# Half-row Toeplitz products of two images side by side, with even and odd lags under one weight tile

## The chip, the cores and the metric

The kernel runs on one core of one Trainium2 chip. The metric is the device time of the whole kernel in microseconds (us). Times of single instructions are given in nanoseconds (ns). All data are f32.

The engines are TensorE (PE; its weight loads are listed apart as PEld), VectorE (DVE), ScalarE (ACT), GpSimd (POOL) and SyncE (SP, which here only issues transfers).

## The reference

Eight images of 128 channels and 32 x 32 pixels go through two layers. Layer 0 is an attention over rows and then a spectral unit along the 1024 pixels taken as a sequence. Layer 1 is a deformable convolution of three taps and then a mixture of eight experts. The part that matters here is the spectral unit. Cut to its core, it is

```python
# u: (8 images, 1024 tokens, 128 channels), normalised; phi: 16 filters over time
U_plus[k]  = causal_convolution(phi[:, k], u)
U_minus[k] = sgn * causal_convolution(phi[:, k], u * sgn)      # sgn = +1, -1, +1, ...
out = sum_k sigma[k] ** 0.25 * (U_plus[k] @ Mpp[k] + U_minus[k] @ Mpm[k])
out = out + sum_lag shift(u, lag) @ Mu[lag]                      # three lags
# four such outputs with their own matrices, over the first 1024, 512, 256 and 128 tokens,
# added with weights from a softmax
```

The alternating sign splits a convolution by the parity of the lag. The sum of the two paths is the convolution with the even lags, taken with the matrix Mpp + Mpm, and the convolution with the odd lags, taken with Mpp - Mpm. An output token of one parity gets its even lags from input tokens of the same parity and its odd lags from the other parity. So all of it is done on sequences of 512 tokens: one parity of one image each.

## The kernel before

**The stages.** The attention comes first (`attention_bounded`; about the first 1018 us of the profiled execution), then a short preparation, and then `spectral_and_second_layer`, to the end. The latter works through four groups of two images. For each group it runs the 16 filters, and between the products it places steps of other work: the second layer of the group before (`layer.image`) and the normalisation of the next group (`spec.prepare`). The images of the last group have their second layer at the end, alone.

**The order is written out by hand.** In `spectral_and_second_layer` each engine executes in the order in which the Python code emits. The other work is a generator, `behind`; each `next` on it emits one step, and it is advanced 1.8 times (`RATE`) at each of eight places per filter. Each filter's products run while the products of the filter before are mixed.

**One filter's products** (`filter_image`, L1148 to L1158). The filter lies in SBUF as a Toeplitz tile `teto` of 128 rows: row p, column c holds phi[p + c - 127] of one parity of lags (L1045 to L1055). The 512 columns for the even lags come first and the 513 for the odd lags behind them. For one image, one output parity (`par`) and one parity of lags (`term`), four matmuls accumulate in one PSUM bank `pu`: the weights are the 128-token block i of the normalised input `ur`, and the moving operand is the first 512 - 128 i columns of the filter, written to the columns from 128 i on. So the matmuls have 512, 384, 256 and 128 columns. In each of them the first 128 columns are the diagonal block of the Toeplitz matrix, half of which is zeros: among these, one quarter is a whole block of 64 x 64 zeros. ScalarE then copies the bank to `us` (L1158). The pool of `pu` has two banks, used in turn.

**The mixing** (`mix`, L1160 to L1165, through `add`, L1141). The copied product of the filter before is multiplied by the filter's 128 x 128 matrices and accumulates in `po`, four banks that hold a group's sums over all filters. The matrices differ over four stretches of tokens (`SPANS`), so a mix has four matmuls with 2 x 64, 2 x 64, 2 x 128 and 2 x 256 columns, of two images at once.

**A round.** One filter is four rounds: (par, term) = (0,0), (0,1), (1,0), (1,1). Within a round the order on TensorE is: product of the first image, the three short spans of the mix, steps of other work, product of the second image, the long span, steps of other work. Each round has its own `us` tile (a pool of six).

**The preparation of a group** (`prepare`, L1083 to L1113). For each image: an indirect DMA from GpSimd's queue fetches the tokens, VectorE takes their statistics, GpSimd computes the inverse deviation in 13 small instructions, VectorE writes the normalised tokens `ur`, and TensorE transposes them for the three lags of `Mu`. For the first group all of it lies ahead of the first product.

Of the kernel before, what the change touches and what calls it, by code (L numbers as in the profile page):

```python
# [9 lines left out]
F32 = mybir.dt.float32  # L10
# [6 lines left out]
P = 128  # L17
B = 8
C = 128
T = 1024  # L20
NT = T // P
HT = T // 2
# [3 lines left out]
NF = 16  # L26
# [5 lines left out]
PHI_ROW = PHI_PAD + 1 + HT  # L32
GROUPS = ((0, 1), (2, 3), (4, 5), (6, 7))
RATE = 1.8
# [3 lines left out]
SPANS = ((0, 64, 4), (64, 128, 3), (128, 256, 2), (256, 512, 1))  # L38
# [613 lines left out]
def norm_steps(nc, sb, src, dst, eps):  # L652

    st = sb.tile([P, NT, 6], F32, tag="st", name="st", bufs=2)
    mv = sb.tile([P, NT, 2], F32, tag="mv", name="mv", bufs=2)
    for i in range(NT):
        nc.vector.bn_stats(st[:, i, :], src[:, i, :])
        nc.vector.bn_aggr(mv[:, i, :], st[:, i, :])
        if i % 2:
            yield  # L660
    rs = inverse_std(nc, sb, mv[:, :, 1], eps)
    for _ in range(3):
        yield
    for i in range(NT):
        nc.vector.tensor_scalar(
            dst[:, i, :], src[:, i, :], mv[:, i, 0:1], rs[:, i : i + 1],
            ALU.subtract, ALU.mult,
        )
        if i % 4 == 3:
            yield  # L670


class DeformAndExperts:
# [90 lines left out]
    def bank(self, name):  # L764
        return self.ps.tile([P, 512], F32, tag="ps", name=name)
# [244 lines left out]
class Spectral:  # L1010
# [34 lines left out]
    def load_filter(self, k):  # L1045


        t = self.sb.tile([P, 2 * HT + 1], F32, tag="teto", name="teto", bufs=3)
        self.nc.sync.dma_start(
            t[:, 0:HT], bass.AP(self.phi_e.tensor, k * PHI_ROW, [[1, P], [1, HT]])  # L1050
        )
        self.nc.sync.dma_start(
            t[:, HT:], bass.AP(self.phi_o.tensor, k * PHI_ROW, [[1, P], [1, HT + 1]])
        )
        return t[:, 0:HT], t[:, HT:]  # L1055

    def load_matrices(self, k, first):

# [25 lines left out]
    def prepare(self, group, bank):  # L1084

        nc, sb = self.nc, self.sb
        for n, b in enumerate(group["images"]):
            if n == 0:
                group["x1"], group["ur"] = [], []
                ut = group["ut"] = sb.tile([C, 2, 2, HT + 1], F32, tag="ut", name="ut")  # L1090
                nc.gpsimd.memset(ut[:, :, :, 0:1], 0.0)
            x1 = sb.tile([P, NT, C], F32, tag="x1", name="x1", bufs=2)
            nc.gpsimd.indirect_dma_start(
                out=x1.rearrange("p i c -> p (i c)"), out_offset=None,
                in_=self.x1d.rearrange("b p i c -> (b p) (i c)"),
                in_offset=bass.IndirectOffsetOnAxis(ap=self.back[:, b : b + 1], axis=0),
            )
            ur = sb.tile([P, NT, C], F32, tag="ur", name="ur", bufs=4)
            group["x1"].append(x1)
            group["ur"].append(ur)  # L1100
            yield
            yield
            yield from norm_steps(nc, sb, x1, ur, 1e-5)
            yield
            for par in range(2):
                pt = bank("p_ut")
                for i in range(4):
                    nc.tensor.matmul(
                        pt[:, i * P : (i + 1) * P], ur[:, par * 4 + i, :], self.flip,
                        start=True, stop=True,  # L1110
                    )
                nc.scalar.copy(ut[:, n, par, 1 : HT + 1], pt)
                yield  # L1113
# [30 lines left out]
        )  # L1144
        group["opened"].add(bank)

    def filter_image(self, group, n, par, term, teto, us):

        nc = self.nc
        src = par if term == 0 else 1 - par  # L1150
        flt = teto[0] if term == 0 else teto[1][:, par : par + HT]
        pu = self.up.tile([P, HT], F32, tag="u", name="pu")
        for i in range(4):
            nc.tensor.matmul(  # L1154
                pu[:, i * P : HT], group["ur"][n][:, src * 4 + i, :], flt[:, 0 : HT - i * P],
                start=(i == 0), stop=(i == 3),
            )
        nc.scalar.copy(us[:, n, :], pu)  # L1158

    def mix(self, group, par, term, spans, mf, us, last):  # L1160
        for lo, hi, k in spans:
            self.add(
                group, (par, lo // 256), self.span(group, par, lo, hi), mf[:, k - 1, term, :],
                us[:, 0 : len(group["images"]), lo:hi], last and term == 1,
            )  # L1165

    def finish(self, group):
# [9 lines left out]
def spectral_and_second_layer(tc, spec, layer):  # L1177
    groups = [{"images": im} for im in GROUPS]
    for _ in spec.prepare(groups[0], layer.bank):
        pass  # L1180
    work = [(g, k) for g in range(len(groups)) for k in range(NF)]
    loaded = {}

    def load(n):
        if n < len(work):
            g, k = work[n]
            loaded[n] = spec.load_filter(k), spec.load_matrices(k, g == 0)

    behind, done, todo = iter(()), 0, 0.0
    load(0)  # L1190
    load(1)
    before = None
    for n in range(len(work) + 1):
        now = work[n] if n < len(work) else None
        if now is not None and now[1] == 1:

            g = now[0]
            tasks = [layer.image(b, groups[g - 1]["x2"][:, m]) for m, b in
                     enumerate(groups[g - 1]["images"])] if g else []
            if g + 1 < len(groups):  # L1200
                tasks.append(spec.prepare(groups[g + 1], layer.bank))
            behind = chain(*tasks)
        sums = {}
        for i in range(4):
            par, term = divmod(i, 2)
            if now is not None:
                group = groups[now[0]]
                us = spec.sb.tile([C, 2, HT], F32, tag="us", name="us", bufs=6)
                sums[i] = us
            for m in range(2):  # L1210
                if now is not None and m < len(group["images"]):
                    spec.filter_image(group, m, par, term, loaded[n][0], us)
                if before is not None and before[1] == 0 and i + m == 0:
                    spec.start_sums(groups[before[0]])
                if before is not None:
                    spec.mix(
                        groups[before[0]], par, term, SPANS[0:3] if m == 0 else SPANS[3:4],
                        loaded[n - 1][1], kept[i], before[1] == NF - 1,
                    )
                todo += RATE  # L1220
                while todo >= 1:
                    todo -= 1
                    next(behind, None)
        if before is not None and before[1] == NF - 1:
            for _ in behind:
                pass
            spec.finish(groups[before[0]])
        load(n + 2)
        kept, before = sums, now
    runs = [layer.image(b, groups[-1]["x2"][:, m]) for m, b in enumerate(groups[-1]["images"])]  # L1230
    alive, step = [], 0
    while runs or alive:
        if runs and step % STAGGER == 0:
            alive.append(runs.pop(0))
        alive = [r for r in alive if next(r, r) is not r]
        step += 1
# [3 lines left out]
def metaformer_kernel(  # L1240
# [33 lines left out]
    with tc.manual_schedule(engines=None):  # L1274
        spectral_and_second_layer(tc, spec, layer)
# [50 lines left out]
```

## Time and profile before

| | us |
|---|---|
| median of three runs | 3162.05 |
| lowest and highest | 3161.14, 3165.78 |
| span of the profiled execution | 3164.1 |
| TensorE busy | 2788.8 |
| of it the products, L1154 | 1206.0 |
| of it the mixing, L1142, with `us` and `mf` | 530.6 |
| ScalarE, copies of the products, L1158 | 299.6 |

The table is from the first part of the page (busy time of each engine) and from its fifth (groups of instructions by line). Each f32 matmul of the program is executed as two instructions, each with its own load of weights, so counts of instructions are twice those in the code: L1154 has 2048 matmuls and 4096 instructions. The mean granted clock of TensorE was 0.951. The first product starts at 1060.66 us, and the last product's records start at 2918 us.

The array form of a matmul is printed ahead of its shape: 128*128 uses the whole array, 64*128 half of its rows, 32*128 a quarter of its rows, 128*32 a quarter of its columns.

### The profile page before, as it was taken

The numbers are of one execution on the slowest core, as the hardware profiler recorded it, in microseconds if no ns is written. First come the engines' busy times: TensorE is split into PE (matmuls) and PEld (weight loads), VectorE is DVE, ScalarE is ACT, GpSimd is POOL, SyncE is SP. The second block draws the span as 40 slices with busy tenths as digits, with TensorE's granted clock in tenths as the row PEclk, the third lists the DMA queues.
The fourth block names the chain that finished last, engine by engine and source line by source line (L and its number), as shares of the span: only waits on it lengthen the run. The fifth ranks groups of instructions, "written<-read, shape, count | busy, mean of one in ns | idle before, by whom it ended". The sixth has DMA issues, their size and how long they took to land.

```text
span 3164.1 us, 45167 instructions
## 1 busy us (share of the span) xinstructions
PE 2788.8 (88%) x18888; PEld 1709.7 (54%) x18888; DVE 1430.6 (45%) x2908; ACT 977.2 (31%) x1152; POOL 958.0 (30%) x876
## 2 busy tenths in 40 slices
PE   5898998998997699999999999989899989899154
PEld 2454454454553466666566566656566656566022
DVE  1677778777787320000243531153332144241477
ACT  2665656666664121111212112211212211211100
POOL 1666666666775210000210300120200030200331
PEclk9999999999999799999999999999999999999566
DMA  0000000000000422221520611331611241510541
GB/s 24 8 8 8 15 3 14 15 2 8 9 8 14 119 67 61 72 62 40 154 73 30 204 40 60 119 108 34 197 36 54 87 140 47 170 57 14 159 133 40
DMA packets 176724, 198.76 MB, mean 63 GB/s; under 512 B 17205, under 2 KB 135157, under 8 KB 176513
## 3 DMA queue, kind: packets, MB, share of 16 engines
q1 hardware_dynamic: 160000, 141.26, 15.0%
q0 software_dynamic: 16512, 54.54, 5.8%
q8 instruction: 150, 2.46, 0.3%
q14 instruction: 62, 0.50, 0.0%
HBM read 127.83 MB, written 67.92 MB: 62 GB/s over the span
## 4 chain that ended last, share of the span: by engine, by line
PE 80%; ACT 7%; DVE 7%; issue 3%; DMA 1%; POOL 1%; SPq 1%; another core or an unknown queue 1%; POOLq 0%; DVEq 0%; ACTq 0%
PE pu L1154 35%; PE po L1142 16%; PE s L509 9%; ACT e L514 6%; PE av L561 4%; PE p_e L927 3%; PE z L530 3%; DVE x L909 2%; PE rb L544 2%; PE p_g L856 1%; PE pk L478 1%; DVE x L933 1%; PE pq L464 1%; DVE e L551 1%
## 5 line engine op out<-in xcount | busy, mean ns | idle before, releaser
L1154 PE MATMUL pu<-teto,ur 128*128 128x512 f32 (+3 forms) x4096 | 1206.0, 438 | 53.5 <-issue 42.3
L1154 PEld LDWEIGHTS pu<-teto,ur 128*128 128x128 f32 x4096 | 779.3, 192 | 606.2 <-issue 417.4
L1158 ACT COPY us<-pu 128x512 f32<-128x512 f32 x512 | 299.6, 585 | 1351.2 <-PE pu L1154 1199.0
L523 POOL TENSOR_TENSOR t<-e 128x1024 f32<-128x1024 f32 x256 | 607.0, 2372 | 356.3 <-ACT e L514 354.1
L551 DVE TENSOR_TENSOR e<-e,rb 128x2048 f32<-128x2048 f32 x256 | 569.6, 2281 | 119.3 <-PE rb L544 119.3
L514 ACT ACTIVATE e<-s 128x2048 f32<-128x2048 f32 x256 | 480.8, 1878 | 277.3 <-PE s L509 255.0
L1142 PE MATMUL po<-us,mf 128*128 128x128 f32 (+2 forms) x2048 | 530.6, 382 | 0.0
L509 PE MATMUL s<-q,k 32*128 32x256 f32 x4096 | 301.1, 409 | 75.9 <-ACT e L514 75.7
L894 POOL DMA_INDIRECT g<-tab,cn_idx x192 | 184.9, 963 | 438.6 <-DMA teto<-in_phi_e 240.8
L643 POOL TENSOR_SCALAR rs_v<-rs_v 128x8 f32<-128x8 f32 x24 | 5.9, 246 | 1020.3 <-DVE rs_b L641 1020.3
L509 PEld LDWEIGHTS s<-q,k 32*128 32x128 f32 x4096 | 188.9, 188 | 203.0 <-ACT e L514 165.8
L561 PE MATMUL av<-e,vt 128*32 128x256 f32 x4096 | 277.6, 389 | 4.0 <-DVE e L551 2.7
L1142 PEld LDWEIGHTS po<-us,mf 128*128 128x128 f32 x2048 | 272.0, 193 | 4.1 <-issue 3.9
L909 DVE SCALAR_TENSOR_TENSOR x<-g,w,x 128x128 f32<-128x128 f32 x704 | 248.0, 352 | 51.3 <-DVE x L909 24.2
L933 DVE SCALAR_TENSOR_TENSOR x<-p_e,gates,x 128x128 f32<-128x128 f32 x512 | 177.1, 350 | 171.2 <-PE p_e L927 154.6
L561 PEld LDWEIGHTS av<-e,vt 128*32 128x32 f32 x4096 | 107.9, 110 | 136.4 <-issue 76.3
L537 DVE RECIPROCAL r<-z 128x256 f32<-128x256 f32 x64 | 112.4, 1757 | 98.4 <-PE z L530 98.1
L927 PE MATMUL p_e<-ew,tc 128*128 128x512 f32 x256 | 137.5, 650 | 15.8 <-DVE x L933 12.7
L1076 DVE TENSOR_SCALAR mf<-both,coef 128x256 f32<-128x256 f32 x16 | 5.6, 353 | 290.8 <-PE po L1142 246.2
L530 PE MATMUL z<-t,group 128*32 128x256 f32 x2048 | 135.4, 382 | 0.0
L878 DVE TENSOR_TENSOR om<-p_om,base 128x72 f32<-128x72 f32 x8 | 1.9, 231 | 240.3 <-PE p_om L873 240.3
L1174 DVE COPY x<-po 128x512 f32<-128x512 f32 x8 | 5.5, 692 | 221.3 <-ACT x L1174 221.3
(199 smaller groups left out, 1607.5 us busy)
## 6 DMA issues: line engine op xcount, KB each, us to landing
tab<-gs SPq DMA_DIRECT2D x192, 256.0 KB
mf<-mfd SPq DMA_DIRECT2D x48, 512.0 KB
teto<-in_phi_o SPq DMA_DIRECT2D x64, 256.5 KB
teto<-in_phi_e SPq DMA_DIRECT2D x64, 256.0 KB
mfd<-mf SPq DMA_DIRECT2D x16, 512.0 KB
xc<-in_x SPq DMA_DIRECT2D x8, 512.0 KB
x1d<-xt SPq DMA_DIRECT2D x8, 512.0 KB
mp<-in_M_plus SPq DMA_DIRECT2D x16, 256.0 KB
```

What stands on the lines that cost most here:

```text
L509: nc.tensor.matmul(s[:, j, c, :], img["k"][rows, hg, 2 * r + c, :], q[rows, qc * QU : (qc + 1) * QU], start=True, stop=True,)
L514: nc.scalar.activation(e.rearrange("p j c q -> p (j c q)"), s.rearrange("p j c q -> p (j c q)"), AF.Exp, scale=float(HD) ** -0.5,)
L523: nc.gpsimd.tensor_add(t, e[:, :, 0, :], e[:, :, 1, :])
L530: nc.tensor.matmul(un["z"][32 * j : 32 * j + 32, 0:QU], group, un["t", r][:, j, :], start=(r == 0), stop=(r == 3), skip_group_check=True,)
L551: nc.vector.tensor_tensor(e, e, un["rb"].unsqueeze(2).to_broadcast([P, NH, 2, QU]), ALU.mult)
L561: nc.tensor.matmul(qrt["av"][32 * j : 32 * j + 32, 0:QU], img["v"][:, 2 * r + c, P * hg + 32 * j : P * hg + 32 * j + 32], un["e", r][:, j, ...
L909: nc.vector.scalar_tensor_tensor(x3[:, i, :], g[:, k * C : (k + 1) * C], w[:, i, tap, k : k + 1], (tok if tap + k == 0 else x3)[:, i, :], ...
L927: nc.tensor.matmul(pe, tc[:, i * P : (i + 1) * P], self.ew[:, grp * 4 : grp * 4 + 4, :].rearrange("d e c -> d (e c)"), start=True, stop=True,)
L933: nc.vector.scalar_tensor_tensor(x3[:, i, :], pe[:, k * C : (k + 1) * C], gate[:, i, grp * 4 + k : grp * 4 + k + 1], x3[:, i, :], ALU.mult ...
L1142: self.nc.tensor.matmul(out, lhsT, rhs, start=bank not in group["opened"], stop=last, skip_group_check=True)
L1154: nc.tensor.matmul(pu[:, i * P : HT], group["ur"][n][:, src * 4 + i, :], flt[:, 0 : HT - i * P], start=(i == 0), stop=(i == 3),)
L1158: nc.scalar.copy(us[:, n, :], pu)
```

## The change

A product is no longer made for one image, one output parity and one parity of lags, but for one image, one *source* parity and both parities of lags: the same block of `ur` as weights, and as moving operand a view of `teto` with two stretches of columns, the even lags and the odd lags. The first gives output of the source's own parity, the second output of the other parity. So that both stretches have one distance, the tile is one column longer. A bank `pu` holds 2 x 256 columns: both terms, of one half of the 512 tokens. So a unit (`filter_unit`) is made per source parity and half, four per filter, and each makes both images.

Within each diagonal block the first 64 output columns need 64 of the 128 rows only. These are now matmuls of half height, 2 x 64 columns each. For the second image of a group they use rows 64 to 127 of `ur` and of `teto`. For the first image a copy of rows 64 to 127 of its `ur` is kept in rows 0 to 63 of a new tile `low`, which GpSimd writes once per group, and `teto` is read 64 columns further on in rows 0 to 63, where the same values stand. So the two images' half-height matmuls use different halves of the array's rows and different banks. The remaining columns of each bank get matmuls of full height. A unit's order on TensorE is four half-height matmuls (block, image: first, second, first, second), then the full ones of the first image, steps of other work, the full ones of the second image, steps of other work, and then both mixes, the short spans and the long, of one term of the filter before.

Per filter there were 32 product matmuls with 10240 columns. There are now 24 of full height with 8192 columns and 16 of half height with 128 columns each. The copies by ScalarE stay eight per filter at 512 columns. The mixes, and the number of places for steps of other work, stay. `us` is now one tile per source parity with both terms (a pool of three at twice the size).

```diff
     def load_filter(self, k):
-        t = self.sb.tile([P, 2 * HT + 1], F32, tag="teto", name="teto", bufs=3)
+        t = self.sb.tile([P, 2 * HT + 2], F32, tag="teto", name="teto", bufs=3)
...
+                group["low"] = sb.tile([64, NT, C], F32, tag="low", name="low", bufs=2)
...
             yield from norm_steps(nc, sb, x1, ur, 1e-5)
             yield
+            if n == 0:
+                nc.gpsimd.tensor_copy(group["low"], ur[64:P])
...
-    def filter_image(self, group, n, par, term, teto, us):
+    def filter_unit(self, group, src, half, filters, us):
         nc = self.nc
-        src = par if term == 0 else 1 - par
-        flt = teto[0] if term == 0 else teto[1][:, par : par + HT]
-        pu = self.up.tile([P, HT], F32, tag="u", name="pu")
-        for i in range(4):
-            nc.tensor.matmul(
-                pu[:, i * P : HT], group["ur"][n][:, src * 4 + i, :], flt[:, 0 : HT - i * P],
-                start=(i == 0), stop=(i == 3),
-            )
-        nc.scalar.copy(us[:, n, :], pu)
+        lags = filters[:, 0 : 2 * (HT + 1 - src)].rearrange("p (a c) -> p a c", a=2)
+        images = range(len(group["images"]))
+        pus = [self.up.tile([P, 2, HT // 2], F32, tag="u", name="pu") for _ in images]
+        for i in (2 * half, 2 * half + 1):
+            to = (i % 2) * P
+            for n in images:
+                low = group["low"][0:64] if n == 0 else group["ur"][n][64:P]
+                rows, c0 = (slice(0, 64), 64) if n == 0 else (slice(64, P), 0)
+                nc.tensor.matmul(
+                    pus[n][:, :, to : to + 64], low[:, src * 4 + i, :],
+                    lags[rows, :, c0 : c0 + 64], start=(i % 2 == 0), stop=False,
+                    skip_group_check=True,
+                )
+        for n in images:
+            for i in range(2 * half + 2):
+                to = (i % 2) * P + 64 if i // 2 == half else 0
+                c0 = to + (2 * half - i) * P
+                nc.tensor.matmul(
+                    pus[n][:, :, to:], group["ur"][n][:, src * 4 + i, :],
+                    lags[:, :, c0 : c0 + HT // 2 - to], start=False, stop=(i == 2 * half + 1),
+                    skip_group_check=True,
+                )
+            nc.scalar.copy(us[:, :, n, half * (HT // 2) : (half + 1) * (HT // 2)], pus[n])
+            yield
...
+        for src in range(2):
+            if now is not None:
+                sums.append(spec.sb.tile([C, 2, 2, HT], F32, tag="us", name="us", bufs=3))
+            for half in range(2):
+                unit = iter(())
+                if now is not None:
+                    unit = spec.filter_unit(groups[now[0]], src, half, loaded[n][0], sums[src])
+                for m in range(2):
+                    next(unit, None)
+                    todo += RATE
+                    while todo >= 1:
+                        todo -= 1
+                        next(behind, None)
                 if before is not None:
-                    spec.mix(
-                        groups[before[0]], par, term, SPANS[0:3] if m == 0 else SPANS[3:4],
-                        loaded[n - 1][1], kept[i], before[1] == NF - 1,
-                    )
+                    group = groups[before[0]]
+                    if before[1] == 0 and src + half == 0:
+                        spec.start_sums(group)
+                    for spans in (SPANS[0:3], SPANS[3:4]):
+                        spec.mix(
+                            group, src, half, spans, loaded[n - 1][1], kept[src],
+                            before[1] == NF - 1,
+                        )
```

## The prediction

> **What bounds the kernel now.** I read the page first: the busy line, the slices and the chain.
>
> ```profile
> PE 2788.8 (88%) x18888; PEld 1709.7 (54%) x18888; DVE 1430.6 (45%) x2908; ACT 977.2 (31%) x1152; POOL 958.0 (30%) x876
> ...
> L1154 PE MATMUL pu<-teto,ur 128*128 128x512 f32 (+3 forms) x4096 | 1206.0, 438 | 53.5 <-issue 42.3
> ```
>
> TensorE is busy 88% of the span, and the row of the Toeplitz products, L1154, is the largest. The chain of waits gives 35% of the span to L1154 and 16% to L1142, the mixing matmuls. Cut into stretches, the stage that the change touches runs from 1060 to 2915 us, and TensorE is busy 1799 of these 1855 us. Here time is the sum of what TensorE executes, plus some waits, all in L1154. The timeline of TensorE in one quiet filter, with the start and the length of each merged run:
>
> ```profile
> 1303.57 1.04 PE L1142 MATMUL po<-us,mf 128*128 128x128 f32 x6
> 1304.45 2.32 PE L1154 MATMUL pu<-teto,ur 128*128 128x512 f32 x8
> 1306.61 1.02 PE L1142 MATMUL po<-us,mf 128*128 128x512 f32 x2
> ```
>
> Start to start, one call of filter_image takes 2.16 us (1304.45 to 1306.61), the short mix 0.88, the long mix 0.86. The lengths are larger because their ends overlap the next run. Each f32 matmul appears as two instructions, so 2 x 1280 columns took 2.16 us: 0.844 ns per column and instruction. A filter is four rounds of two calls and two mixes: 24.2 us, of which 8 x 2.156 = 17.25 us is L1154. The work is 64 filters.
>
> The change makes half-height matmuls in this stage, which has none. The attention stage has some (L544, array form 64*128), between 128*32 before and 128*128 after:
>
> ```profile
> 265.30 1.07 PE L561 MATMUL av<-e,vt 128*32 128x256 f32 x16
> 266.30 1.13 PE L544 MATMUL rb<-r,spread 64*128 64x256 f32 x8
> 267.37 1.12 PE L464 MATMUL pq<-hk,wq 128*128 128x512 f32 x2
> ```
>
> The eight of L544 start in four pairs, 7 ns apart within a pair, one on each half of the rows. Four pairs at 256 x 0.844 = 0.216 us are 0.864 us, but the next form starts 1.07 us after them: 0.206 us is extra. And the two 512-column instructions of L464 last 1.12 us together where L1142's last 1.02: 0.10 extra. Start times of single instructions, over all changes of form in the trace with nothing else to wait for, split this: 92 to 96 ns from the end of the last stream to the first load of weights in the new form, and then 107 ns in which this first load is not hidden. The 48 changes from 64*128 to 128*128 have a median of 93 ns.
>
> **What the Trainium skill says.** "TensorEngine Tiling (Array Packing)", section Key Properties: a change of tiling mode drains TensorE. The trace agrees, with the 92 to 96 ns. "TensorE: Matmul & The Clock Gate", section LDWEIGHTS: a load takes its columns over 1.2 GHz, whatever its rows, so 107 ns for 128. The trace agrees: 107 ns exposed for 32, 64 and 128 rows alike. The same page, Part 3: matmuls on different row groups run at the same time, and a load overlaps a running matmul only if its row group differs or it goes to the background buffer. The pairs of L544 agree.
>
> **The change part by part.** *Columns.* Before, each of 8 calls per filter streams 512+384+256+128 = 1280 columns: 10240. After, per source half and image, the full-height matmuls have 512 columns in half 0 (384+128) and 1536 in half 1 (512+512+384+128); times two images and two sources: 8192. The half-height ones have 128 columns and pair up over two images: 4 per unit, 4 units, so 16, or 8 pairs of 128, 1024 columns of time. Total 9216: 1024 fewer columns x 2 instructions x 0.833 ns (the bare stream: a 512-column step takes 0.429 us, a 128-column step 0.109, and the difference is 0.320 for 384 columns) = 1.71 us per filter, 109 us for 64. This is what the change gives if nothing else is added.
>
> *Changes of form.* Each unit enters 64*128 and leaves it. In: 93 ns drain above the usual step, plus 104 of load. Out: 96 (with the 7 ns stagger of the pair) plus 104. Sum 0.40 us per unit, 1.59 per filter. The step from 128*128 into 64*128 itself isn't in the trace; from 128*128 to 32*128 and from 128*32 to 64*128 both show it, so I take their value.
>
> *Sum of the stream.* After: 8192 x 2 x 0.833 ns = 13.65, 48 instructions with 2.6 to 5 ns between = 0.16; 16 pair steps at 0.112 us (128-column steps of L1142 take 0.109 to 0.112) = 1.79; form changes 1.59. Sum 17.19 against 17.25: 0.06 to 0.08 us less per filter, 5 us in 64. With pair steps of 0.107 to 0.118 us and changes of 0.38 to 0.42 us per unit, it lies between 13 us less and 6 more. So the saving and the drains cancel.
>
> *Slack of the two pu banks.* Before, a call takes one bank, and the bank is wanted again after two mixes and another call, 3.9 us. After, a unit's half-height pairs write both banks first, so it waits for ScalarE's copy of the second image, which ends 0.90 us after that image's last matmul starts (1306.49 to 1307.39). Two mixes, 1.74 us, hide that, except in the first filter of all, which has none: four waits of about 0.75, 3 us. But where ScalarE is late, the hiding fails:
>
> ```profile
> 1572.50 2.32 PE L1154 MATMUL pu<-teto,ur 128*128 128x512 f32 x8
> 1574.65 1.04 PE L1142 MATMUL po<-us,mf 128*128 128x128 f32 x6
> 1582.53 4.36 PE L1154 MATMUL pu<-teto,ur 128*128 128x512 f32 x8 [6.83 <-issue]
> ```
>
> The copy due near 1571.9 ran at 1581.89 (ScalarE idle 12.45 us, "issue"), and TensorE ran on for 3.9 us before it stopped. Ten such waits of over 2 us lie between 1090 and 2915. With the change TensorE runs on for 1.74 us when the second image's copy is late, or about 3.5 when the first's is and it must then wait for both copies: 1.1 to 2.2 us worse each. Ends 0 and 22 us; I take 8, as some delays will fall beside other waits.
>
> *Places of the other layer's steps.* Same number (8 places, 14.4 steps per filter), but the places were 3.03 us apart and are now from 0.86 us (two images in half 0) to about 5. TensorE and ScalarE are in order, so a step put 0.86 us after the one that it needs may hold them. Before, no wait of this kind shows in the stage. Ends 0 and 12; I take 4.
>
> *The low copy and the start.* For the first group it stands on GpSimd's queue ahead of the second image's fetch. Before: fetch at 1042.74, first image normalised at 1047.00, second image's statistics from 1049.20, first product at 1060.66. After: the copy can't start before 1047.00; I price 64x1024 at 1.5 us, between the 0.96 of a 128x1024 memset and the 2.34 of an addition. The fetch then follows at 1048.5 and, with the first image's 4.7 us from fetch to statistics, the second's start near 1053.2: 4 us later (ends 3 and 6). In groups 2 to 4 it hides behind some 450 us of products.
>
> *Boundaries, buffers.* Opening a group's sums waited three times 0.70 us for L1174's copies; a whole unit now stands ahead: minus 1 (ends minus 2, 0). Eight ScalarE copies of 585 ns per filter and the loads remain, behind TensorE's 24 us; us keeps its 24 KB per row.
>
> Total: -5 +3 +8 +4 +4 -1 = +13 us on the profiled 3164.1. The unprofiled median is 3162.05, so 3175.
>
> **The rivals.** *Exact balance.* Late copies and crowded steps cost nothing: -5 +3 +4 -1, near 3163. For it: in the stretch 1090 to 1524 TensorE idles under 1 us of 434. Against: the ten waits. *Cheaper changes of form (faster).* TensorE loads the first weights of the new form while the old one still streams, as it does within a form. Half-height loads touch half of the rows only, which speaks for it; the 48 changes out of 64*128 with 107 ns exposed speak against it. If both loads are hidden, a unit saves 0.21 us, 256 units 53 us: 3175 - 53 = 3122. It wins over the lost slack from about 0.05 us per unit, a change priced under 0.35 instead of 0.40. *Pairs in series.* The half-height matmuls of the two images don't overlap: 0.45 us more per unit, 115 us: 3290. L544's pairs, in the same order of halves, speak against it.
>
> **How the numbers follow.** Forecast (slack lost) 0.58, exact balance 0.21, cheaper changes 0.13, series 0.08. About 0.2%, 6 us, is what a measurement can tell from no change. Faster is the third case, 0.13; same the second, 0.21; slower the first and last, 0.66. The forecast's own range is -10 to +44: 3152 to 3206. Adding the balance, and the near end of the third case, 3146 to 3206 leaves out about 2 in 10.
>
> **What would show it.** In the quiet stretch after the first filter, a filter should again take 24.1 to 24.2 us. A unit should show pairs 7 ns apart, 0.09 us of nothing and 0.107 us of bare load on both sides. The idle time ahead of the half-height matmuls should be 10 to 20 us above the 53.5 of L1154, with the ScalarE copy as its releaser. The first product should start near 1064.7. A filter of 23.4 us or less in the quiet stretch would prove the price of the changes wrong; one of 26, the pairs.

## The result and the profile after

The changed kernel takes 3204.59 us (median of four runs, 3195.70 to 3208.97) against 3161.60 for the kernel before (four runs, 3159.01 to 3165.78). The ratio is 1.0131, with a 95% interval of 1.0107 to 1.0155: 43 us slower. The profiled execution spans 3194.0 us, 29.9 more than that of before, and is the fastest of the four.

The page of the changed kernel, parts 1 and 5: busy time, then the groups of the products (matmuls in the last three lines).

```profile
PE 2791.2 (87%) x19912; PEld 1636.8 (51%) x19912; DVE 1427.4 (45%) x2908; ACT 973.8 (30%) x1152; POOL 962.8 (30%) x880
...
L1175 PE MATMUL pu<-teto,ur 128*128 128x384 f32 (+2 forms) x3072 | 977.1, 464 | 0.0
...
L1166 PE MATMUL pu<-teto,low 64*128 64x128 f32 x1024 | 188.5, 303 | 44.4 <-issue 39.0
L1166 PE MATMUL pu<-teto,ur 64*128 64x128 f32 x1024 | 185.4, 302 | 23.4 <-issue 22.3
```

TensorE is as busy as before, with 1024 instructions more. The full-height products, L1175, never wait. All idle time of the products stands before the half-height ones, L1166, which open each unit. There are 67.8 us of it (44.4 + 23.4), where L1154 had 53.5. The changes of form are not in it: in a quiet filter, below, no idle time is shown beside them, because the modelled end of each matmul reaches over the change.

The timeline of TensorE in one quiet filter of the changed kernel (start, length, merged run; of the second and the third pair the first line alone):

```profile
1300.64 0.37 PE L1166 MATMUL pu<-teto,low 64*128 64x128 f32 x1
1300.65 0.37 PE L1166 MATMUL pu<-teto,ur 64*128 64x128 f32 x1
1300.86 0.27 PE L1166 MATMUL pu<-teto,low 64*128 64x128 f32 x1
1300.97 0.27 PE L1166 MATMUL pu<-teto,low 64*128 64x128 f32 x1
1301.08 0.27 PE L1166 MATMUL pu<-teto,low 64*128 64x128 f32 x1
1301.09 0.27 PE L1166 MATMUL pu<-teto,ur 64*128 64x128 f32 x1
1301.29 5.43 PE L1175 MATMUL pu<-teto,ur 128*128 128x512 f32 x16
1306.56 1.90 PE L1146 MATMUL po<-us,mf 128*128 128x128 f32 x8
1308.39 0.37 PE L1166 MATMUL pu<-teto,low 64*128 64x128 f32 x1
```

The pairs run side by side. The first pair takes 0.22 us to the next, the others 0.11: the first load of weights is bare. After the last pair 0.20 us pass to L1175, for 0.107 us of stream, and the mixes take 1.83 us where 0.88 + 0.86 = 1.74 stood before: both are the drain. Over the entries with no other wait (some 250 of 256) the median time from the end of the last stream to the new form is 95 ns, and the bare load is 106 ns. On the way out it is 94 and 106. A quiet filter takes 24.13 us from start to start, and it took 24.21.

So the stream of work is where it was, and the 30 us must be elsewhere. The next table cuts the profiled executions by the starts of instructions in the trace: the attention ends with the start of its last L561 matmul, a filter goes from its first product to the next filter's first product, and the last row begins with the start of the last mixing matmul. "Gather filters" are the 12 filters in which the second layer of the six images of groups 1 to 3 fetches its rows (two per image); in a kernel without waits they take as long as quiet ones. The two columns on the right are for later: they are the same two programs in the experiments, on two different chips (the kernel before on chip 12, the changed one on chip 10).

| us | before | after | difference | before, chip 12 | after, chip 10 |
|---|---|---|---|---|---|
| to the end of the attention | 1015.7 | 1012.4 | -3.4 | 1013.0 | 1013.3 |
| from there to the first product | 44.9 | 53.2 | +8.3 | 44.5 | 53.6 |
| first filter | 17.3 | 19.4 | +2.1 | 17.8 | 20.5 |
| 14 quiet filters | 339.0 | 337.8 | -1.2 | 339.0 | 337.8 |
| 12 gather filters | 367.3 | 391.8 | +24.5 | 290.6 | 289.6 |
| the other 37 filters | 1141.4 | 1144.5 | +3.1 | 1141.4 | 1144.5 |
| after the last mix | 238.3 | 234.9 | -3.4 | 231.9 | 232.8 |
| span | 3164.1 | 3194.0 | +29.9 | 3078.2 | 3092.0 |

Most of the loss is in the gather filters, where the kernel before already lost 77 us against quiet ones. The longest case in the changed kernel, TensorE and then ScalarE:

```profile
2280.59 2.00 PE L1175 MATMUL pu<-teto,ur 128*128 128x384 f32 x8
2282.43 1.90 PE L1146 MATMUL po<-us,mf 128*128 128x128 f32 x8
2299.06 0.79 PE L1166 MATMUL pu<-teto,low 64*128 64x128 f32 x2 [14.73 <-issue]
```
```profile
2279.31 0.58 ACT L1180 COPY us<-pu 128x512 f32<-128x512 f32 x1 [3.73 <-remote]
2298.43 1.29 ACT L1180 COPY us<-pu 128x512 f32<-128x512 f32 x2 [18.53 <-remote]
```

ScalarE makes no copy from 2279.9 to 2298.43, and then both of the unit at once. TensorE finishes the unit and the mixes by 2284.3 and stands still for 14.73 us. The profile puts the wait down to "issue", but it ends at 2299.06, when the first of the two copies (0.58 us, from 2298.43) has just ended. Summed over the stage (waits of TensorE between 1090 and 2835 us: total us, times, longest us), first the kernel before, then the changed one:

```profile
PE pu L1154 <- issue: 42.3, 9, 8.4
PE pu L1154 <- ACT us L1158: 11.2, 3, 8.6
```
```profile
PE pu L1166 <- issue: 61.3, 10, 14.7
PE po L1146 <- issue: 8.1, 7, 2.3
PE pu L1166 <- ACT us L1180: 5.4, 1, 5.4
```

Before the products 53.5 us became 66.7, which is 13.2 more. Another 8.1 us stand before mixing matmuls. They lie inside two runs of mixes (2079.9 to 2084.1 and 2578.4 to 2584.7 us), whose matmuls start 1.4 to 2.8 us apart there. No bank is waited for: ScalarE executes nothing from 2069.9 to 2089.9 or from 2569.9 to 2589.9 us, and these mixes go on without it. So whatever held ScalarE may have held TensorE too. Without the waits, the gather filters took 313.8 us before (367.3 - 53.5) and 317.0 after (391.8 - 74.8), against 290.6 and 289.6 in the two columns on the right: 23.2 and 27.4 us went into slower running. The clock is lower there: between 1560 and 1610 us the granted clock was 0.90 in the kernel before and 0.86 in the changed one. So the 24.5 us are 13.2 and 8.1 of waits, 4.2 of slower running, and 1.0 less of stream.

### The profile page after: what moved, and what is told of

It is laid out like the page before. It is cut to its first block, busy times and chain, and to the rows that moved or that the text cites. A ratio compares the mean times of both kernels' runs of the same rounds, so it can differ in the third digit from the quotient of the medians.

```text
span 3194.0 us, 47045 instructions
## 1 busy us (share of the span) xinstructions
PE 2791.2 (87%) x19912; PEld 1636.8 (51%) x19912; DVE 1427.4 (45%) x2908; ACT 973.8 (30%) x1152; POOL 962.8 (30%) x880
## 4 chain that ended last, share of the span: by engine, by line
PE 57%; DVE 5%; issue 3%; another core or an unknown queue 1%; SPq 1%; DMA 1%; POOL 0%; ACT 0%; POOLq 0%; DVEq 0%; ACTq 0%
PE pu L1175 29%; PE po L1146 16%; PE pu L1166 5%; PE p_e L927 3%; DVE x L909 2%; DVE x L933 2%; PE p_g L856 1%; SPq L864 1%; PE p_turn L772 1%; PE p_l L971 0%; PE p_out L944 0%; PE p_out L947 0%; PE p_ut L1112 0%; DMA g<-tab,cn_idx 0%
## 5 line engine op out<-in xcount | busy, mean ns | idle before, releaser
L1175 PE MATMUL pu<-teto,ur 128*128 128x384 f32 (+2 forms) x3072 | 977.1, 464 | 0.0
L1175 PEld LDWEIGHTS pu<-teto,ur 128*128 128x128 f32 x3072 | 537.7, 192 | 437.5 <-issue 273.6
L1146 PE MATMUL po<-us,mf 128*128 128x128 f32 (+2 forms) x2048 | 490.4, 382 | 8.1 <-issue 8.1
L1146 PEld LDWEIGHTS po<-us,mf 128*128 128x128 f32 x2048 | 294.2, 192 | 42.1 <-issue 28.4
L561 PE MATMUL av<-e,vt 128*32 128x256 f32 x4096 | 276.6, 388 | 5.5 <-DVE e L551 4.2
L1166 PEld LDWEIGHTS pu<-teto,low 64*128 64x128 f32 x1024 | 136.0, 189 | 238.4 <-issue 229.4
L1166 PE MATMUL pu<-teto,low 64*128 64x128 f32 x1024 | 188.5, 303 | 44.4 <-issue 39.0
L1166 PE MATMUL pu<-teto,ur 64*128 64x128 f32 x1024 | 185.4, 302 | 23.4 <-issue 22.3
L561 PEld LDWEIGHTS av<-e,vt 128*32 128x32 f32 x4096 | 107.7, 110 | 137.0 <-issue 75.1
L1166 PEld LDWEIGHTS pu<-teto,ur 64*128 64x128 f32 x1024 | 135.6, 190 | 26.1 <-issue 24.0
```

The lines of the kernel that those rows point to most:

```text
L561: nc.tensor.matmul(qrt["av"][32 * j : 32 * j + 32, 0:QU], img["v"][:, 2 * r + c, P * hg + 32 * j : P * hg + 32 * j + 32], un["e", r][:, j, ...
L1146: self.nc.tensor.matmul(out, lhsT, rhs, start=bank not in group["opened"], stop=last, skip_group_check=True)
L1166: nc.tensor.matmul(pus[n][:, :, to : to + 64], low[:, src * 4 + i, :], lags[rows, :, c0 : c0 + 64], start=(i % 2 == 0), stop=False, skip_g ...
L1175: nc.tensor.matmul(pus[n][:, :, to:], group["ur"][n][:, src * 4 + i, :], lags[:, :, c0 : c0 + HT // 2 - to], start=False, stop=(i == 2 * h ...
```

## Experiments

My theory was that the stream balances, as the quiet filters show, and that the loss is slack: a unit needs both banks of `pu` at its start, so TensorE runs on for a shorter time when a ScalarE copy is late. The rival was that steps of other work, which now stand 0.9 to 5 us apart and not 3 us, hold TensorE and ScalarE throughout. The start was a matter of its own.

The experiments ran on two chips, 10 and 12, on which the kernel before takes 3079 to 3081 us and has none of the long waits. So each is compared with runs of the kernel before on its own chip. Which chip the first comparison ran on is not known, nor whether another chip or another occasion made the 80 us between the two levels.

### Without the gathers

```diff
-                g = sb.tile([P, 4 * C], F32, tag="g", name="g", bufs=9)
-                nc.gpsimd.indirect_dma_start(out=g, in_=rows, in_offset=...)
-                fetched[i].append(g)
+                fetched[i].append(self.still)
```

`still` is a tile that a memset fills once.

The kernel before:

> The kernel before without the 192 indirect gathers of the second layer: VectorE reads a tile filled once instead, so the sampled values are left out. All theories: TensorE's ten long waits (about 50 us between 1090 and 2915 us) lie in the gather phases. If the gathers make ScalarE's copies late, they vanish and the time falls by 50 to 75 us, to about 3090 to 3110. If something else makes them late (fetching of instructions, VectorE), they stay and the time falls by less than 20.

The changed kernel:

> The changed kernel without the same 192 gathers (the sampled values are left out). Lost slack: the difference to the kernel before without gathers is only what the rest of the prediction's sum gives, -5 stream, +5 start, +3 first filter, at most +4 crowded places, so 2 to 8 us instead of about 40. Crowded places as the main cost: the difference stays at 25 us or more.

The kernel before without gathers took 3062.28 us, 0.9944 (0.9927 to 0.9960) of its 3079.18. The changed kernel without them took 3071.48. The first expectation failed. The 17 us come from the end of the kernel (210.2 us after the last mix against 231.9), less a start that is 6.4 us longer (50.9 against 44.5), and the 12 gather filters take 290.6 us with gathers and without. On this chip the gathers cost the products nothing, so this run can't tell what makes ScalarE late in the first comparison. The second expectation was missed by a little: the distance is 9.2 us (expected 2 to 8, and 25 or more for the rival). The run alone doesn't decide against the rival, as there were no long waits to take away. What does is the row of the other 37 filters in the table: there the changed kernel takes 3.1 us more, in the first comparison and in the experiments alike, where the stream alone gives 3.0 less. So crowded places cost about 6 us there, and they are not the main cost.

### The changed kernel again, and both with ScalarE made late

> The changed kernel as it is, beside the kernel before, to see it on a chip together with the next two. Where the gather phases hold no long waits: 8 to 12 us slower than before (start 5 to 8, first filter 3, stream -5, crowded places the rest). Where they do, as in the first comparison: 35 to 45 us slower.

It took 3091.28 us against 3080.68, a ratio of 1.0038 (1.0024 to 1.0051): 10.6 us slower, as expected where no long waits occur. The waits of TensorE, of the changed kernel on this chip:

```profile
PE p_back L960 <- DVE x L1198: 2.0, 3, 0.7
PE p_e L927 <- DVE x L933: 1.7, 4, 0.5
```

After the first filter no wait for ScalarE is left, and the table's last column shows that the gather filters take 289.6 us. So the change costs 43 us in the first comparison and 11 here. To see whether late copies can make that difference, they were made late by hand, in both kernels (`idle` is a tile that a memset fills once):

```diff
             if i + 2 < NT:
                 fetch(i + 2)
+            if i in (1, 5):
+                for _ in range(14):
+                    nc.scalar.copy(self.idle, self.idle)
```

> The kernel before with ScalarE made late on purpose: 14 extra copies of 128x512, about 8 us, at two steps of the gather phase of every image (12 such blocks in the stage of the products, 4 in the tail). TensorE runs on for about 3.9 us, so each block costs 2 to 4.5 us in the stage: 25 to 55 us more than the kernel before.

> The changed kernel with the same 14 extra copies at the same steps. Lost slack: TensorE runs on for 1.7 to 3.5 us only and then waits for both copies, so each block costs 1 to 2.2 us more than in the kernel before: the distance between the two is 12 to 26 us above the distance between the plain kernels on this chip. If slack is not what the change loses: the same distance as between the plain kernels, within 5 us.

The kernel before rose to 3143.85 us, by 63.2, which is above the expected 25 to 55. The changed kernel rose to 3189.18, by 97.9. The distance between them went from 10.6 to 45.3 us, the size seen in the first comparison. It is 34.7 us more, above the expected 12 to 26. One block in the kernel before, on ScalarE and then on TensorE:

```profile
1574.00 9.07 ACT L911 COPY idle<-idle 128x512 f32<-128x512 f32 x14
1582.97 1.07 ACT L1163 COPY us<-pu 128x512 f32<-128x512 f32 x2
```
```profile
1577.15 2.32 PE L1159 MATMUL pu<-teto,ur 128*128 128x512 f32 x8
1579.31 1.04 PE L1147 MATMUL po<-us,mf 128*128 128x128 f32 x6
1583.60 2.42 PE L1159 MATMUL pu<-teto,ur 128*128 128x512 f32 x8 [3.25 <-ACT us L1163]
```

And the same block in the changed kernel:

```profile
1573.82 9.07 ACT L911 COPY idle<-idle 128x512 f32<-128x512 f32 x14
1582.80 0.58 ACT L1185 COPY us<-pu 128x512 f32<-128x512 f32 x1
```
```profile
1573.95 1.90 PE L1151 MATMUL po<-us,mf 128*128 128x128 f32 x8
1575.79 0.48 PE L1171 MATMUL pu<-teto,low 64*128 64x128 f32 x2
1583.43 0.58 PE L1171 MATMUL pu<-teto,ur 64*128 64x128 f32 x1 [7.16 <-ACT us L1185]
```

ScalarE is occupied for 9.07 us in both. After the product whose copy is delayed (1574.14 to 1576.3), the kernel before goes on with a mix, one more product and another mix, and waits 3.25 us. The changed kernel goes on with its two mixes, stops at the first pair, whose second half needs the second image's bank, and waits 7.16 us. Over the 12 blocks of the stage, before and after:

```profile
PE pu L1159 <- ACT us L1163: 38.7, 12, 3.2
```
```profile
PE pu L1171 <- ACT us L1185: 66.4, 12, 7.2
```

That is 2.3 us of waiting more per block, (66.4 - 38.7) / 12. Not all of it is slack, because the copies aren't equally late. Counted from the end of the product's last matmul, the first delayed copy of a block starts 6.5 us later in the kernel before. In the changed kernel it is 4.3 to 8.7 us, 7.3 on average: its copies don't come 3 us apart, and most blocks fall closer ahead of one. That is 0.8 us per block, and 1.5 are left for the slack.

The gather filters grew by more than the waits: by 56.2 us in the kernel before (290.6 to 346.8) and by 97.9 in the changed one (289.6 to 387.5), a difference of 41.7. (The whole kernels differ by less, 34.7, since with the extra tile the start became 5.7 us longer in the kernel before and 1.6 shorter in the changed one.) The rest, 17.5 and 31.5 us, is what runs slower afterwards: full-height matmuls of a unit that took 5.43 us take 6.60 after the wait of 7.16, while after the 3.25 us a product takes 2.42 in place of 2.32. Between 1583 and 1592 us the granted clock was 0.78 in the changed kernel and 1.00 in the kernel before.

### Another order within a unit

If the wait for both banks at the start of a unit is the cause, an order that needs the second bank later must give the time back. The first image's full-height matmuls were put first, then the pairs, then the second image's. The matmuls and the changes of form are the same.

```diff
+        full(0)                      # full-height matmuls of the first image
         for i in (2 * half, 2 * half + 1):
             for n in images:
                 nc.tensor.matmul(...)    # half height
         for n in images:
-            full(n)
+            if n == 1:
+                full(1)
             nc.scalar.copy(us[:, :, n, ...], pus[n])
```

> The changed kernel with the 14 extra ScalarE copies, and another order within a unit: the first image's full-height matmuls first (they need its bank alone), then the half-height pairs, then the second image's. Same matmuls, same two changes of form. Lost slack: TensorE runs on for 1.7 us plus 0.9 or 2.6 us more before it needs the second bank, near the 3.9 of the kernel before, so each block costs about as in before_late: the idle time before the products falls from 66 us to 38 to 48, and the time by 20 to 40 us against after_late, to about 3150 to 3170 on a chip like that one. If the wait for both banks isn't the cause: no change, within 5 us.

It took 3159.56 us against 3079.90 for the kernel before on its chip, 79.7 above it. In the order of the change it had been 108.5 above (3189.18 - 3080.68). So the order alone gives back about 29 us, within the expected 20 to 40, and 21.7 of them lie in the gather filters (387.5 to 365.8). The two lines of waits add to 47.6 us, at the upper end of the expected 38 to 48:

```profile
PE pu L1182 <- ACT us L1190: 34.7, 8, 4.4
PE pu L1170 <- ACT us L1190: 12.9, 4, 4.1
```

L1170 are the first image's full-height matmuls, L1182 the pairs. Eight of the 12 waits now come behind the former. The copies are as late as in the changed kernel (7.3 us on average), so these 18.8 us of waiting (66.4 - 47.6), 1.6 per block, are slack alone. This shows that the order in which a unit needs its banks sets a large part of what a late copy costs: the matmuls and the changes of form stayed the same.

### The half-height matmuls undone

```diff
-        for i in (2 * half, 2 * half + 1):
...
-                nc.tensor.matmul(pus[n][:, :, to : to + 64], low[:, src * 4 + i, :], ...)
...
-                to = (i % 2) * P + 64 if i // 2 == half else 0
+                to = (i % 2) * P if i // 2 == half else 0
```

The first full-height matmul of an image now opens its bank (`start`); the diff doesn't show that line.

> The changed kernel with its half-height matmuls undone: full-height matmuls cover the diagonal blocks, so no changes of form, 10240 columns per filter, and a unit first needs only the first image's bank; order of places, mixes, views and the low copy as in the change. Lost slack: 24.2 us per quiet filter, long waits as in the kernel before, so the kernel before plus the start's 5 us and at most 5 more, 3165 to 3172. Crowded places: 3190 to 3205, as in the changed kernel.

It took 3084.29 us against 3079.18: 1.0018 (1.0011 to 1.0025), 5.1 us slower. The expectations were put on the level of the first comparison; on this chip slack says 3084 to 3089 (the kernel before plus 5 to 10), which fits. The rival's 25 us and more can't show here, where the changed kernel itself is only 11 us behind, so the run doesn't decide between the two. The 5.1 us are the start, which is 7.4 longer than that of the kernel before (51.9 against 44.5), less what the filters give. The quiet filter, two units with their mixes:

```profile
1296.07 6.18 PE L1165 MATMUL pu<-teto,ur 128*128 128x512 f32 x16
1302.08 1.90 PE L1146 MATMUL po<-us,mf 128*128 128x128 f32 x8
1303.82 2.74 PE L1165 MATMUL pu<-teto,ur 128*128 128x512 f32 x8
1306.40 1.90 PE L1146 MATMUL po<-us,mf 128*128 128x128 f32 x8
```

The units take 6.01 and 2.58 us here. In the changed kernel they take 5.92 and 2.49, but each pair of mixes 0.09 more. The filter is 24.13 us in both. So the zero quarters are worth just what the changes of form cost. The 0.08 us that the change gains on the kernel before stay without half-height matmuls, so they come from the shared weight tile, with 24 matmuls in place of 32, and not from the zeros.

### The start

> The changed kernel with the low copy behind the second image's fetch on GpSimd's queue. If the copy delays the first product, this gives back 4 to 5 us: first product near 1061 and about 3200. If the first product is late for another reason, nothing changes.

```diff
-            if n == 0:
-                nc.gpsimd.tensor_copy(group["low"], ur[64:P])
...
+            if n == 1:                   # behind the second image's fetch
+                nc.gpsimd.tensor_copy(group["low"], group["ur"][0][64:P])
```

GpSimd in the changed kernel, the low copy and the fetch behind it:

```profile
1046.58 1.03 POOL L1108 COPY low<-ur 64x1024 f32<-64x1024 f32 x1 [2.84 <-issue]
1047.89 1.06 POOL L1094 DMA_INDIRECT x<-x1d,back  x1 [0.28 <-POOL low L1108]
```

With the copy moved (same view):

```profile
1039.70 1.05 POOL L1094 DMA_INDIRECT x<-x1d,back  x1 [0.16 <-issue]
1044.27 1.03 POOL L1101 COPY low<-ur 64x1024 f32<-64x1024 f32 x1 [3.51 <-DMA x<-x1d,back]
```

The time is 3084.14 us, 1.0020 (1.0013 to 1.0026) of the kernel before, where the changed kernel is 1.0038. From the end of the attention to the first product it takes 47.0 us in place of 53.6: 6.6 back, a little more than the expected 4 to 5. The last 2.5 us above the 44.5 of the kernel before stay.

The traces show why. The order of the constants' loads and small operations in this part isn't written out by hand, and it differs between the programs. VectorE has one operation that waits nearly 5 us for a load of a bias, first in the kernel before, then in the changed one:

```profile
1044.00 0.23 DVE L716 TENSOR_TENSOR base<-base,bias 128x72 f32<-128x72 f32 x1 [4.96 <-DMA bias<-in_off_b]
```
```profile
1036.64 0.23 DVE L716 TENSOR_TENSOR base<-base,bias 128x72 f32<-128x72 f32 x1 [4.83 <-DMA bias<-in_mask_b]
```

In the kernel before it stands behind the first image's statistics, where it holds up nothing. In the changed kernel, and in every version with the low copy, it stands among them. So the second image's fetch starts 27.0 us after the end of the attention in the kernel before and 35.5 in the changed one: 4.3 of the 8.5 us are there before the low copy comes, and the other 4.2 are the copy, for which GpSimd stands idle 2.84 us, until the last tokens are normalised, and which then takes 1.03. With the copy moved, the fetch starts at 30.5. This part is easily upset: where only a tile and a memset had been added to the kernel before (the late-copies version), it took 50.2 us.

### Versions meant to gain

The order of units and the moved copy together:

> The changed kernel with that order, without extra copies, and with the low copy behind the second image's fetch. Quiet filters 24.13 us as before; start 5 us earlier, first filter 1 to 2 us shorter. On a chip without long waits within 3 us of the kernel before; on one with them 30 us faster than the changed kernel.

It took 3082.80 us against 3079.90: 1.0010 (1.0003 to 1.0016). The quiet filter is 24.12 us and the start 48.2, as expected; the first filter is 17.3, 3.2 shorter than in the changed kernel, where 1 to 2 were expected. It is the best form with half-height matmuls, and on this chip it is still not faster than the kernel before. On a chip with long waits it was not run.

The shared views alone, without the low copy:

> The changed kernel with full-height diagonal blocks and without the low copy: the shared views of even and odd lags alone. Quiet filters 24.13 us against 24.21, start as in the kernel before: 2 to 5 us faster than the kernel before, at the edge of what can be told.

It took 3080.68 us: 1.0004 (0.9996 to 1.0012). The 2 to 5 us aren't there. Quiet and gather filters gave 2.1 us; the start took 0.8 and the tail 1.1 us more than in the profile of the kernel before on this chip.

The kernel before with the first group's two images prepared in turn, step by step:

> The kernel before, with the preparation of the first group's two images interleaved, so that the second image's fetch no longer queues behind the first image's GpSimd chain. If that chain sets the first product, it comes 5 to 10 us earlier and the kernel is 0.15 to 0.3% faster than before; if the loads of the other constants set it, nothing changes.

It took 3080.99 us against 3080.68: 1.0001 (0.9993 to 1.0010). The start took 45.5 us, though the second image's fetch started 11 us earlier (15.7 us after the attention in place of 27.0). That fetch alone doesn't set the first product.

And the kernel before, profiled on one of these chips for the table:

> The kernel before, profiled on the same chip, to compare stages. On a chip without long waits its start (end of the attention to the first product) is near 45 us and no wait of the products is over 1 us in the gather phases.

3079.91 us; its start took 44.5 us, and its only wait of the products' kind is the one at the opening of a group's sums:

```profile
PE po L1142 <- PE pu L1154: 2.1, 3, 0.7
```

No version that does all of the work beat the kernel before.

## Why the prediction was right, and where it was off

The direction was right and the time, 3204.59, lies in the range, 1.4 us from its upper edge (3206) and 30 us from the 3175 forecast. That it fell inside is in part luck: without late copies the same change costs 10.6 us, close to the 13 forecast, but made up otherwise: 9.1 us for the start in place of 4, and nothing for late copies in place of 8. Step by step:

- **Columns and changes of form.** 24.1 to 24.2 us per quiet filter was predicted, 24.13 measured. The prices read from L544 held: 95 ns and 106 ns each way, and pairs in 0.11 us. The step from 128*128 to 64*128, which the trace of before didn't have, costs what its neighbours cost. The statements taken from the Trainium skill agree with these numbers: the drain at a change of mode ("TensorEngine Tiling (Array Packing)", Key Properties), and the load at its columns over 1.2 GHz, 107 ns ("TensorE: Matmul & The Clock Gate", LDWEIGHTS). The two rivals on this term, cheaper changes of form and pairs in series, fell. So did exact balance, near 3163: even where no copy is late the change costs 10.6 us.
- **Slack of the two banks.** The mechanism was right: with copies made late it gives 1.5 to 1.6 us per block, inside the 1.1 to 2.2 that were priced. Its size was taken too low: 8 us, with ends of 0 and 22. In the first comparison the waits before the products grew by 13.2 us, inside these ends, and the gather filters by 24.5, just outside. What the sum left out are the slower running after a longer wait (4.2 us there; 1.2 us per block, (31.5 - 17.5) / 12, with copies made late) and 8.1 us of waits inside the mixes, which slack doesn't explain. The idle time ahead of the half-height matmuls rose by 14.3 us (53.5 to 67.8), within the 10 to 20 that were named as a sign, but the profile puts most of it down to "issue" and not to the ScalarE copy.
- **Low copy and start.** 4 us predicted (3 to 6), 8.3 measured. The term itself was right: the copy puts the fetch off by 4.2 us (it took 1.03 us, less than the 1.5 assumed). What was missed is that the order of the operations around it would change too, so that VectorE waits for a bias in the middle of the first image's statistics, 4.3 us more.
- **First filter.** 3 us predicted, 2.1 and 2.7 in the two pairs of profiles in the table.
- **Crowded places.** 4 us predicted (0 to 12). The other 37 filters should have gained 3.0 us at 0.08 each and lost 3.1, so this cost about 6. With full-height matmuls they take 1141.3 us, so some 3 of the 6 belong to the half-height ones.
- **Boundaries.** 1 us less was predicted. It is too small to be told from the rest.

In the profiles the sum is 29.9 us where 13 was forecast. The gather filters took 16.5 us more than the 8 put down for slack, the start 4 more and the crowded places 2 more, against 3.4 each that attention and tail happened to be shorter. Between the medians the difference is 43 us. The other 13 us are in executions that no profile shows; the runs of the changed kernel spread over 13 us, and those of the kernel before over 7.

What stays open is why ScalarE's copies come up to 17 us late in the gather phases of the first comparison. The profile gives no releaser ("issue", "remote"), and the two chips of the experiments don't show it, so it couldn't be tried there. That late copies cost the changed order more was shown with copies that were late for a known reason. That the 24.5 us of the first comparison have this cause is argued from the same pattern in its two traces, one per kernel, and not shown: image by image the two gather filters lose from 1.0 us less to 9.1 us more than before, the copies are not late by the same amount in both, and 8.1 us stand where no bank is waited for.

## What to carry to other kernels

Price a half-array matmul with the two changes of form around it: here 0.40 us per visit, which needs 240 full-array columns of f32 saved (0.40 us / 1.67 ns per column over both instructions) before it pays. When two buffers are filled by one unit and not in turn, work out how long the producer can run on if their consumer is late, and put first the work that needs one buffer only. A copy added to a queue costs what stands behind it: look for the next transfer on that queue. And where the order of the operations isn't written out by hand, look whether it is still the same: here that cost as much as the copy.

## What the runs showed that was not expected

- The same program took 3161.6 us in the first comparison, whose chip isn't known, and 3079 to 3081 on chips 10 and 12. In the profiles 77 of the 86 us lie in the 12 gather filters (367.3 against 290.6 us), where ScalarE's copies come late. So a change that costs 11 us on one occasion costs 43 on another.
- A wait of 7.16 us left TensorE slow for some time after: the full-height matmuls behind it took 6.60 us in place of 5.43. After one of 3.25 us the product took 2.42 in place of 2.32.
- A change of form costs much the same in nearly every direction: medians of 91 to 96 ns from the end of the last stream, and the load of the first weights bare (106 to 107 ns at 128 columns, 27 at 32). The exception is the step from 64*128 to 32*128 in the attention: 120 ns in 12 of 14 cases. Why is not known.
